# Attention on one NeuronCore: the value product of a group in one TensorE run instead of two

## The chip, the cores and the metric

The kernel runs on one core of a Trainium2 chip. The metric is device time in microseconds (us) from launch to end. The kernel before took 1688.72 us, the median of three runs (1685.79 to 1690.38). One further execution was taken with the hardware profiler; all durations below come from it.

The engines are TensorE (PE, matmuls; its weight loads are shown as PEld), VectorE (DVE), ScalarE (ACT), GpSimd (POOL) and SyncE (SP, which here only issues transfers). TensorE writes to PSUM, eight banks of 512 float32 columns on 128 partitions. DVE and ACT read it there.

## The reference

One layer in float32: cross attention, a sparsified gated feed-forward part, and a low-rank mixture of experts, each with a layer norm before it and a residual. The change is in the cross attention:

```python
xq = q.reshape(b, s, N_KV_HEADS, N_REP, HEAD_DIM)        # 16 x 64 tokens, 8 x 4 heads of 32
scores = jnp.einsum('bsgrd,btgd->bgrst', xq, xk) / math.sqrt(HEAD_DIM)   # t = 1601
probs = jax.nn.softmax((scores + mask).astype(jnp.float32), axis=-1)
out = jnp.einsum('bgrst,btgd->bsgrd', probs, xv)
x = x + out
```

Here q is the layer norm of x, and keys and values are both the context. The feed-forward part has a width of 2752 and keeps the larger half of the gate's magnitudes; eight experts of rank 16 follow, two per token.

## The kernel before

**Groups.** Attention is cut into 64 groups: batch element b (16), half h of the eight key heads (2), half rh of the four query heads that share a key head (2). A group has four key heads g, each of 32 dimensions. For each the 128 partitions of a score tile are 2 query heads x 64 tokens, and the columns are the 1601 context rows. Eight groups (two batch elements) use one tile of 128 tokens; the index of a group inside its tile is m.

**Steps of a group** (class `Group`). `scores(d)` computes half d of the columns (0 to 801, 801 to 1601) for the four heads as eight matmuls: a part of 512 columns for each head, then a part of 289 or 288. The four heads lie on different 32-row strips of the array and stream side by side. Seven results go to banks of the pool `ps_t`, which has seven and hands them out in rotation; the last goes to the bank `shared`. `masked(d)` is eight DVE operations that add the mask and write to SBUF, with a running maximum; each is followed by a short read of the accumulator. After d=1 a reduction makes the negative maximum `nm`. `softmax(g)` is one ACT exponent over 1601 columns with its sum. `turn(heads)` transposes the probabilities of two heads on TensorE, 26 blocks in seven banks of `ps_t`, and returns the seven copies from PSUM to SBUF (`pT`) for the caller to place on ACT or DVE. `values(d)` multiplies transposed probabilities with values: 13 blocks of context rows times four heads on 32-column strips. In the trace each float32 matmul shows as two weight loads and two matmul records, so 104 records for a group. The result `po` is the last 128 columns of the bank `shared`. `keep(d)` copies `po` into `oT` on DVE (d=0) or adds it there (d=1). `inverse` takes the reciprocals of the sums.

**Order.** `InOrder` (line 88) keeps each engine's operations in the order in which the program calls them, so the loop over groups sets every queue by hand. Its helper is line 96, which is why almost all rows of the profile carry L96. In iteration n, for d = 0 and 1, the calls are: scores(d) of group n+1, values(d) of group n-1, masked(d) of n+1, turn of two heads of group n with copies 0, 1, 2, 3 and 5 on ACT and 4 and 6 on DVE, keep(d) of n-1, and two exponents (heads 2 and 3 of n in d=0, heads 0 and 1 of n+1 in d=1). TensorE thus repeats: scores, values, transposes, scores, values, transposes. `values(0)` takes six blocks, `values(1)` seven.

**Beside it.** On SP stand the loads of keys and values (`load_kv`, at the first score run of every fourth group), of the next tile of x (m=2) and its queries (m=3), and the store of a finished tile (m=4). `Norm` computes a token tile's statistics on DVE, half of it at each d of m=4; `row_tile` sends them through DRAM and `scale_queries` (POOL, m=5) makes the queries. `finish_tile` transposes `oT` back and adds it to x. POOL also forms sums of weight blocks, one of 48 units per group. The feed-forward part behind is ordered by a planner (`Plan`) with its own costs. It calls the last group's values, keep and inverse first.

Of the kernel before, what the change touches and what calls it, by code (L numbers as in the profile page):

```python
# [9 lines left out]
F32 = mybir.dt.float32  # L10
# [6 lines left out]
ALU = mybir.AluOpType  # L17
# [3 lines left out]
P = 128  # L21
B, S, D = 16, 64, 1024
T, C = 1601, 256
HD = 32
# [3 lines left out]

HALVES = [(0, 801), (801, T)]
BANK = 512  # L30
LOADS = [(0, 512), (512, 801), (801, T)]
NCH = 4
I = 2752
IC = 344
# [22 lines left out]
def tile_perceiver_layer(  # L57
# [120 lines left out]
    def sums_out(u):  # L178
        (_, t), _ = sum_columns(u)
        pool.dma_start(t, sums[u])  # L180

    def load_x(i, parts=1):
        x[i] = xp.tile([P, D], F32, tag="x", name=f"x{i}")
        for j in range(parts):
            cols = slice(j * D // parts, (j + 1) * D // parts)
            sp_queue.dma_start(x[i][:, cols], x_in[i * P : (i + 1) * P, cols])
# [76 lines left out]
    class Group:  # L263
# [7 lines left out]
        def scores(self, d):  # L271


            b, h, rh = self.b, self.h, self.rh
            if d == 0:
                self.sc = [
                    scp.tile([P, T], F32, tag=f"sc{g}", name=f"sc{g}_{self.name}")
                    for g in range(4)
                ]
                self.mx = small.tile([P, 4, NCH], F32, tag="mx", name=f"mx_{self.name}")  # L280
                self.sums = small.tile([P, 4], F32, tag="sums", name=f"sums_{self.name}")
                if (h, rh) == (0, 1) and b + 1 < B:
                    load_kv(b + 1)
            t0, t1 = HALVES[d]
            mid = t0 + BANK
            self.parts = []
            for j in range(8):
                g, (c0, c1) = j % 4, ((t0, mid), (mid, t1))[j // 4]
                bank = shared
                if j < 7:  # L290
                    bank = ps_t.tile([P, BANK], F32, tag="pt", name=f"ps{j}_{self.name}_{d}")
                ps = bank[:, : c1 - c0]
                rows = slice(g * HD, (g + 1) * HD)
                q = qT[b // 2][rows, h, b % 2, 2 * rh : 2 * rh + 2, :]
                pe.matmul(
                    ps,
                    q.rearrange("p r s -> p (r s)"),
                    kv[b][0][h][rows, c0:c1],
                    start=True,
                    stop=True,  # L300
                )
                self.parts.append((g, c0, c1, ps, 2 * d + j // 4))

        def masked(self, d):

# [40 lines left out]
            copies.append((pT[:TL, :, last, :], pt[:TL]))  # L346
            return copies

        def values(self, d):


            c0, c1 = ((0, NTC // 2), (NTC // 2, NTC), (0, NTC))[d]
            v = kv[self.b][1][self.h]
            for c in range(c0, c1):
                w = min(P, T - c * P)
                for g in range(4):
                    pe.matmul(
                        po[g * HD : (g + 1) * HD, :],
                        v[:w, c, g * HD : (g + 1) * HD],
                        self.pT[g][:w, c, :],  # L360
                        start=(c == c0),
                        stop=(c == c1 - 1),
                    )

        def keep(self, d):

            i, bb = self.b // 2, self.b % 2
            if bb == 0 and self.h == 0 and self.rh == 0 and d != 1:
                oT[i] = otp.tile([P, 2, 4, 2, S], F32, tag="oT", name=f"oT{i}")
                rs_tok[i] = small.tile([P, 2, 4, 4], F32, tag="rs", name=f"rs{i}")  # L370
            rows = oT[i][:, self.h, 2 * self.rh : 2 * self.rh + 2, bb, :]
            new = po.rearrange("p (r s) -> p r s", r=2)
            if d == 1:
                dve.tensor_tensor(rows, new, rows, ALU.add)
            else:
                dve.tensor_copy(rows, new)

        def inverse(self):

# [9 lines left out]
    def finish_tile(i, h, home=ps_t, tag="pt"):  # L389


        if h == 0:
            att[i] = xnp.tile([P, 2, 4, 4, HD], F32, tag="xn", name=f"att{i}")
        rows = att[i][:, h]
        pt = home.tile([P, 4, P], F32, tag=tag, name=f"pto{i}_{h}")
        for r in range(4):
            pe.transpose(
                pt[:, r, :], oT[i][:, h, r].rearrange("p b s -> p (b s)"), ident
            )

        def add():
            pool.tensor_tensor(
                rows, rows, rs_tok[i][:, h].unsqueeze(3).to_broadcast([P, 4, 4, HD]),
                ALU.mult,
            )
            xv = x[i].rearrange("p (h g r d) -> p h r g d", h=2, g=4, r=4)
            pool.tensor_tensor(xv[:, h], xv[:, h], rows, ALU.add)

        return (rows, pt.rearrange("p r (g d) -> p r g d", g=4)), add
# [24 lines left out]
    for d in range(2):  # L434
# [1 line left out]
        for _ in range(4):  # L436
            pe.transpose(po, ident, ident)
        groups[0].masked(d)
    for g in range(2):
        groups[0].softmax(g)  # L440


    first, first_xn = (xnp, otp), {}
    for n in range(ng):
        i, m = n // 8 + 1, n % 8
        group = groups[n]
        last = n == ng - 1
        if m == 2 and i < NT:
            load_x(i)
        if m == 3 and i < NT:  # L450
            raw = load_queries(i)
        if m == 4 and n > 8:
            sp_queue.dma_start(xs[i - 2], x[i - 2])
        if n == ng - 3:
            for j in range(2):
                x[j] = xp.tile([P, D], F32, tag="x", name=f"x{j}_f")
                sp_queue.dma_start(x[j], xs[j])
        for d in range(2):
            add = None
            following = groups[n + 1] if not last else None  # L460
            if following:
                following.scores(d)
            if n > 0:
                groups[n - 1].values(d)
            if following:
                following.masked(d)
            on_act = [0, 1, 2] if last else [0, 1, 2, 3, 5]
            if n > 8 and 3 <= 2 * m + d <= 4:
                copy, add = finish_tile(i - 2, 1 - d)
                act.copy(*copy)  # L470
            if last:
                groups[n - 1].keep(d)
            copies = group.turn((2 * d, 2 * d + 1))
            for j, copy in enumerate(copies):
                if j in on_act:
                    act.copy(*copy)
                else:
                    dve.tensor_copy(*copy)
            if n > 0:
                if not last:  # L480
                    groups[n - 1].keep(d)
                if d == 1:
                    groups[n - 1].inverse()
            for g in range(2):
                if d == 0:
                    group.softmax(2 + g)
                elif following:
                    following.softmax(g)
            if add:
                add()  # L490
            if i < NT:
                if (m, d) == (4, 0):
                    norm = Norm(x[i], f"q{i}", float(HD))
                if m == 4:
                    norm.half(d)
                if (m, d) == (4, 1):
                    norm.end()
                    row = row_tile(i)
                if (m, d) == (5, 1):
                    scale_queries(i, raw, row)  # L500
            if d == 1 and 0 <= n - 3 < 3 * NU:
                sums_made(n - 3)
                sums_out(n - 3)
            if d == 1 and 0 <= n - 2 < 3 * NU:
                sums_in(n - 2)
            if last:
                xn = first[d].tile([P, D], F32, tag=("xn", "oT")[d], name=f"xn_f{d}")
                norm = Norm(x[d], f"f{d}")
                norm.half(0)
                norm.half(1)  # L510
                norm.end()
                dve.tensor_scalar(xn, x[d], norm.mean, norm.rstd, ALU.subtract, ALU.mult)
                first_xn[d] = xn

# [748 lines left out]
    rank = {name: 10 + 10 * j for j, name in enumerate(order)}  # L1265
    gated = [gate(pairs[0], 0, rank["g0"], lambda i: [])]

    t = add("PE", 2.9, lambda: groups[-1].values(2), [], rank["g0"] - 5)
    t = add("DVE", 0.3, lambda: groups[-1].keep(2), [t], 0)
    t = add("DVE", 0.4, lambda: groups[-1].inverse(), [t], 0)  # L1270

    def end():
# [44 lines left out]
class Plan:  # L1317
# [20 lines left out]
    def add(self, engine, cost, emit, deps, rank, takes=None, frees=None, margin=0.0):  # L1338
        holds, frees = (
            [hold for hold in (h if isinstance(h, tuple) else (h,)) if hold]  # L1340
            for h in (takes, frees)
        )
        task = self.Task(engine, cost, emit, deps, rank, holds, margin)
        for hold in frees:
            hold.freed_by = task
        self.tasks.append(task)
        return task
# [102 lines left out]
```

## Time and profile before

| | |
|---|---|
| median of three runs | 1688.72 us |
| the profiled execution's own time | 1688.13 us |
| its span, first to last instruction | 1686.2 us |
| attention, up to the first gate matmul | 814.65 us |
| one group in the steady state | 12.21 us |
| PE, DVE, ACT, POOL busy in 300 to 400 us | 99.95, 90.97, 96.00, 52.71 us |
| granted TensorE clock in that stretch | 1.00 |

A row of the timeline gives the start, the duration, the engine, the line, the operation, output <- input, the shape, and the number of instructions merged into it; in brackets stands the idle time before it and what ended it. PE rows are named by what they write: `ps<-kT,qt` and `shared<-kT,qt` are scores, `shared<-pT,v` values, `pt<-ident,sc` transposes, `pto` the transposes of `finish_tile`. Matmuls are pipelined and their ends modelled, so the distance from one run's start to the next tells more than a duration. ACT's `sc<-sc,nm` is an exponent, `pT<-pt` a copy of transposed probabilities, DVE's `sc<-ps,mask` a masking, `oT<-shared` the work of `keep`.

### The profile page before, as it was taken

What the parts mean: (1) busy time and instruction counts of PE and PEld (TensorE: products, weight loads), DVE (VectorE), ACT (ScalarE), POOL (GpSimd) and SP (SyncE); (2) the same over time, 40 slices, a digit from 0 to 9 for tenths busy, and PEclk for the clock granted to TensorE, in tenths of its full rate; (3) what the DMA queues carried; (4) which work ended last, traced back from release to release, by engine and by line L of the source; (5) the groups of instructions that cost most, each with busy time, mean ns of one, the idle gap of its engine ahead of it and who ended that gap; (6) DMA issues with size and microseconds to landing.
All of it is one profiled execution on the core that took longest, in us unless ns stands there. A gap on an engine that the chain in (4) does not pass through costs nothing. (4 is left out here: it accounts for less than half of the span.)

```text
span 1686.2 us, 38279 instructions
## 1 busy us (share of the span) xinstructions
PE 1662.9 (99%) x15042; PEld 1184.2 (70%) x15042; DVE 1437.8 (85%) x3654; ACT 1257.1 (75%) x1702; POOL 573.9 (34%) x613
## 2 busy tenths in 40 slices
PE   8999999999999999999999999999989999999998
PEld 7888888888888888888666666645645656645644
DVE  7998989999898999988439999999999989999603
ACT  6999999999999999999256675778477772877010
POOL 1055555455554554110221212221480013420631
PEclk9999999999999999999999999999999999999999
DMA  7356657565664766131799999888959979898983
GB/s 220 105 160 202 216 159 228 190 229 169 217 209 155 229 209 201 46 98 49 309 303 327 300 300 305 283 289 266 347 185 302 310 233 328 268 298 270 315 267 133
DMA packets 133586, 389.11 MB, mean 231 GB/s; under 512 B 9888, under 2 KB 61376, under 8 KB 133408
## 3 DMA queue, kind: packets, MB, share of 16 engines
q1 hardware_dynamic: 113840, 315.98, 57.4%
q0 software_dynamic: 19136, 69.61, 12.5%
q8 instruction: 119, 1.95, 0.5%
q10 hardware_dynamic: 432, 1.09, 0.2%
q14 instruction: 59, 0.48, 0.1%
HBM read 344.17 MB, written 42.47 MB: 229 GB/s over the span
## 5 line engine op out<-in xcount | busy, mean ns | idle before, releaser
L96 DVE CUSTOM_DVE_ANT_0 sc<-ps,mask 128x512 f32<-128x512 f32 (+2 forms) x896 | 468.4, 588 | 31.2 <-PE ps L96 30.0
L96 ACT ACTIVATE sign<-a,cand 128x2752 int8<-128x2752 f32 x136 | 351.8, 2587 | 111.5 <-DVE cand L96 111.4
L96 ACT ACTIVATE sc<-sc,nm 128x1601 f32<-128x1601 f32 x256 | 415.7, 1629 | 8.8 <-DVE nm L96 8.8
L96 PE MATMUL pt<-ident,sc 128*128 128x128 f32 (+1 forms) x3328 | 395.1, 275 | 2.1 <-ACT sc L96 1.7
L96 DVE TENSOR_SCALAR_CACHE_REDUCE junk<-a,cand 128x2752 uint8<-128x2752 f32 x124 | 381.7, 3078 | 4.0
L96 PEld LDWEIGHTS pt<-ident,sc 128*128 128x128 f32 (+1 forms) x3328 | 362.7, 141 | 28.4 <-issue 23.8
L96 ACT COPY pT<-pt 128x512 f32<-128x512 f32 x636 | 336.4, 598 | 29.4 <-PE pt L96 17.8
L96 PE MATMUL pg_u<-w_u,hS 128*128 128x344 f32 x896 | 263.4, 452 | 0.0
L96 PE MATMUL pg_g<-w_g,hS 128*128 128x344 f32 x896 | 261.0, 452 | 0.8 <-DVE hS L96 0.8
L96 POOL TENSOR_TENSOR tw<-tw 128x344 f32<-128x344 f32 (+1 forms) x192 | 176.0, 927 | 223.2 <-DMA tw<-in_wg_dram 74.5
L96 PE MATMUL pd<-w_d,s 128*128 128x512 f32 x528 | 234.6, 598 | 0.0
L96 PEld LDWEIGHTS pg_g<-w_g,hS 128*128 128x128 f32 x896 | 169.6, 190 | 88.9 <-DVE hS L96 1.0
L96 PEld LDWEIGHTS pg_u<-w_u,hS 128*128 128x128 f32 x896 | 168.8, 190 | 87.3 <-issue 3.1
L96 PE MATMUL ps<-kT,qt 32*128 32x512 f32 (+2 forms) x1792 | 209.8, 538 | 1.0 <-DVE mx L96 0.9
L96 PE MATMUL shared<-pT,v 128*32 128x128 f32 x6656 | 208.5, 274 | 0.9 <-DVE oT L96 0.7
L96 PEld LDWEIGHTS shared<-pT,v 128*32 128x32 f32 x6656 | 174.2, 110 | 49.6 <-issue 48.0
L96 PEld LDWEIGHTS pd<-w_d,s 128*128 128x128 f32 x528 | 99.6, 193 | 115.7 <-issue 114.8
L96 DVE COPY pT<-pt 128x512 f32<-128x512 f32 (+1 forms) x260 | 139.5, 558 | 38.9 <-PE pt L96 38.9
L96 PEld LDWEIGHTS ps<-kT,qt 32*128 32x128 f32 x1792 | 97.6, 183 | 53.3 <-DVE pT L96 27.8
L96 ACT ACTIVATE s<-s 128x344 f32<-128x344 f32 (+1 forms) x70 | 36.6, 536 | 74.9 <-DVE s L96 74.7
L96 POOL TENSOR_TENSOR s<-s,rank 128x688 f32<-128x688 f32 x32 | 62.4, 1964 | 77.5 <-DVE rank L96 76.9
L96 DVE DVE_READ_ACCUMULATOR2_ANT mx<- 128x1 f32 x1024 | 84.8, 83 | 0.0
(331 smaller groups left out, 1403.2 us busy)
## 6 DMA issues: line engine op xcount, KB each, us to landing
w_g<-ts SPq DMA_DIRECT2D x64, 688.0 KB
w_u<-ts SPq DMA_DIRECT2D x64, 688.0 KB
w_d<-ts SPq DMA_DIRECT2D x48, 768.0 KB
w_g<-in_wg_dram SPq DMA_DIRECT2D x48, 688.0 KB
w_u<-in_wu_dram SPq DMA_DIRECT2D x48, 688.0 KB
w_d<-in_wd_dram SPq DMA_DIRECT2D x36, 768.0 KB
kT<-in_ctx_t_dram SPq DMA_DIRECT2D x31, 800.5 KB
v<-in_ctx_v_dram SPq DMA_DIRECT2D x32, 768.0 KB
```

The lines of the kernel that those rows point to most:

```text
L96: return tc.keep_in_program_order(getattr(self.engine, op)(*args, **kwargs))
```

## The change

- `values` covers all 13 blocks in one call and accumulates them in PSUM; `keep` is one copy, without the addition.
- Order in iteration n: scores(1) and masked(1) of group n+1; turn of heads 2 and 3 of group n; values, keep and inverse of group n; exponents 0, 1 and 2 of n+1; then `next_group(n + 1)`: scores(0) and masked(0) of n+2, turn of heads 0 and 1 of n+1, exponent 3 of n+1. TensorE repeats scores, transposes, values, scores, transposes.
- Copies: of heads 0 and 1, the first six on ACT and the seventh on DVE; of heads 2 and 3, the first four on ACT and three on DVE. In the last group every other one is on ACT.
- In `scores` the parts of 289 or 288 columns come first. The fourth of these goes to `shared`; it is masked last.
- `Norm` of the next tile runs in one piece at m=3, the queries are scaled at m=4; x is loaded at m=1; queries are loaded, and the finished tile is stored, at m=2; `finish_tile` runs at m=0 and 1. The statistics of the first two feed-forward tiles run in the last group but one. The first transfers load columns 512 to 801 ahead of 0 to 512.

```diff
-LOADS = [(0, 512), (512, 801), (801, T)]
+LOADS = [(512, 801), (0, 512), (801, T)]
...
-                g, (c0, c1) = j % 4, ((t0, mid), (mid, t1))[j // 4]
+                g, k, (c0, c1) = j % 4, j // 4, ((mid, t1), (t0, mid))[j // 4]
                 bank = shared
-                if j < 7:
+                if j != 3:
                     bank = ps_t.tile([P, BANK], F32, tag="pt", name=f"ps{j}_{self.name}_{d}")
...
+            self.parts.append(self.parts.pop(3))
...
-            c0, c1 = ((0, NTC // 2), (NTC // 2, NTC), (0, NTC))[d]
             v = kv[self.b][1][self.h]
-            for c in range(c0, c1):
+            for c in range(NTC):
...
-            if d == 1:
-                dve.tensor_tensor(rows, new, rows, ALU.add)
-            else:
-                dve.tensor_copy(rows, new)
+            dve.tensor_copy(
+                oT[i][:, self.h, 2 * self.rh : 2 * self.rh + 2, bb, :],
+                po.rearrange("p (r s) -> p r s", r=2),
+            )
...
+    def next_group(n):
+        if n + 1 < ng:
+            groups[n + 1].scores(0)
+            groups[n + 1].masked(0)
+        turn_and_copy(groups[n], (0, 1), (0, 1, 2, 3, 4, 5))
+        groups[n].softmax(3)
...
+        if following:
+            following.scores(1)
+            following.masked(1)
+        if n >= 8 and m < 2:
+            copy, add = finish_tile(i - 2, m)
+            act.copy(*copy)
+        turn_and_copy(group, (2, 3), (0, 1, 2, 3) if following else (0, 2, 4, 6))
+        if following:
+            group.values()
+            group.keep()
+            group.inverse()
+            for g in range(3):
+                following.softmax(g)
+            next_group(n + 1)
+        if add:
+            add()
+        if i < NT and m == 3:
+            norm = Norm(x[i], f"q{i}", float(HD))
+            for j in range(2):
+                norm.half(j)
+            norm.end()
+            row = row_tile(i)
+        if i < NT and m == 4:
+            scale_queries(i, raw, row)
```

More of the change, by code (lines that the diff above doesn't have):

```diff
@@ L301, in scores @@
                 )
-                self.parts.append((g, c0, c1, ps, 2 * d + j // 4))
+                self.parts.append((g, c0, c1, ps, 2 * d + k))
+            self.parts.append(self.parts.pop(3))
         def masked(self, d):
@@ L347, in turn, with values @@
             return copies
-        def values(self, d):
-            c0, c1 = ((0, NTC // 2), (NTC // 2, NTC), (0, NTC))[d]
+        def values(self):
             v = kv[self.b][1][self.h]
-            for c in range(c0, c1):
+            for c in range(NTC):
                 w = min(P, T - c * P)
@@ L360, in values, with keep @@
                         self.pT[g][:w, c, :],
-                        start=(c == c0),
-                        stop=(c == c1 - 1),
+                        start=(c == 0),
+                        stop=(c == NTC - 1),
                     )
-        def keep(self, d):
+        def keep(self):
             i, bb = self.b // 2, self.b % 2
-            if bb == 0 and self.h == 0 and self.rh == 0 and d != 1:
+            if bb == 0 and self.h == 0 and self.rh == 0:
                 oT[i] = otp.tile([P, 2, 4, 2, S], F32, tag="oT", name=f"oT{i}")
                 rs_tok[i] = small.tile([P, 2, 4, 4], F32, tag="rs", name=f"rs{i}")
-            rows = oT[i][:, self.h, 2 * self.rh : 2 * self.rh + 2, bb, :]
-            new = po.rearrange("p (r s) -> p r s", r=2)
-            if d == 1:
-                dve.tensor_tensor(rows, new, rows, ALU.add)
-            else:
-                dve.tensor_copy(rows, new)
+            dve.tensor_copy(
+                oT[i][:, self.h, 2 * self.rh : 2 * self.rh + 2, bb, :],
+                po.rearrange("p (r s) -> p r s", r=2),
+            )
         def inverse(self):
@@ L438, in tile_perceiver_layer, with turn_and_copy @@
         groups[0].masked(d)
-    for g in range(2):
+    for g in range(3):
         groups[0].softmax(g)
+    def turn_and_copy(group, heads, on_act):
+        for j, copy in enumerate(group.turn(heads)):
+            if j in on_act:
+                act.copy(*copy)
+            else:
+                dve.tensor_copy(*copy)
+    def next_group(n):
[4 more added lines that the diff above has]
+        groups[n].softmax(3)
+    next_group(0)
     first, first_xn = (xnp, otp), {}
@@ L445, in tile_perceiver_layer @@
         i, m = n // 8 + 1, n % 8
-        group = groups[n]
-        last = n == ng - 1
+        group, add = groups[n], None
+        following = groups[n + 1] if n + 1 < ng else None
+        if m == 1 and i < NT:
+            load_x(i)
+        if m == 2 and n > 8:
+            sp_queue.dma_start(xs[i - 2], x[i - 2])
         if m == 2 and i < NT:
-            load_x(i)
-        if m == 3 and i < NT:
             raw = load_queries(i)
-        if m == 4 and n > 8:
-            sp_queue.dma_start(xs[i - 2], x[i - 2])
         if n == ng - 3:
@@ L457, in tile_perceiver_layer @@
                 sp_queue.dma_start(x[j], xs[j])
[L458 to L508, printed above, removed]
@@ new lines, in tile_perceiver_layer @@
+        if following:
[3 more added lines that the diff above has]
+            copy, add = finish_tile(i - 2, m)
+            act.copy(*copy)
+        turn_and_copy(group, (2, 3), (0, 1, 2, 3) if following else (0, 2, 4, 6))
[3 more added lines that the diff above has]
+            group.inverse()
+            for g in range(3):
+                following.softmax(g)
+            next_group(n + 1)
+        if add:
+            add()
@@ new lines, in tile_perceiver_layer @@
+        if i < NT and m == 3:
[6 more added lines that the diff above has]
+            scale_queries(i, raw, row)
+        if 0 <= n - 3 < 3 * NU:
+            sums_made(n - 3)
+            sums_out(n - 3)
+        if 0 <= n - 2 < 3 * NU:
+            sums_in(n - 2)
+        if n == ng - 2:
+            for j in range(2):
+                xn = first[j].tile([P, D], F32, tag=("xn", "oT")[j], name=f"xn_f{j}")
+                norm = Norm(x[j], f"f{j}")
@@ L511, in tile_perceiver_layer @@
                 norm.end()
-                dve.tensor_scalar(xn, x[d], norm.mean, norm.rstd, ALU.subtract, ALU.mult)
-                first_xn[d] = xn
+                dve.tensor_scalar(xn, x[j], norm.mean, norm.rstd, ALU.subtract, ALU.mult)
+                first_xn[j] = xn
     early.close()
@@ L1266, in tile_perceiver_layer @@
     gated = [gate(pairs[0], 0, rank["g0"], lambda i: [])]
-    t = add("PE", 2.9, lambda: groups[-1].values(2), [], rank["g0"] - 5)
-    t = add("DVE", 0.3, lambda: groups[-1].keep(2), [t], 0)
+    t = add("PE", 2.9, lambda: groups[-1].values(), [], rank["g0"] - 5)
+    t = add("DVE", 0.3, lambda: groups[-1].keep(), [t], 0)
     t = add("DVE", 0.4, lambda: groups[-1].inverse(), [t], 0)
```

## The prediction

> **What bounds the kernel now.** I read the page's busy shares first, then busy time by stage, then the timeline of one group, and last the waits. The change lies in attention, which ends with the first gate matmul at 814.65 us; the feed-forward part behind it keeps its code. Busy time in a stretch of 100 us inside attention (columns: PE, weight loads, DVE, ACT, POOL, granted clock, DMA share, GB/s):
>
> ```profile
> PE 1662.9 (99%) x15042; PEld 1184.2 (70%) x15042; DVE 1437.8 (85%) x3654; ACT 1257.1 (75%) x1702; POOL 573.9 (34%) x613
> ...
> 300.00:400.00 100.00, 99.95 (x1524) 83.52 (x1522) 90.97 (x336) 96.00 (x150) 52.71 (x60) 1.00 0.61 200
> ```
>
> TensorE has no idle time, ACT and DVE have little, DMA has plenty. Busy PE alone proves nothing, so here is one group's timeline (start, duration, engine, operation):
>
> ```profile
> 301.16 1.38 PE L96 MATMUL ps<-kT,qt 32*128 32x512 f32 x11
> ...
> 301.61 0.28 DVE L96 TENSOR_TENSOR oT<-shared,oT 128x128 f32<-128x128 f32 x1
> ...
> 301.94 0.18 PEld L96 LDWEIGHTS shared<-kT,qt 32*128 32x128 f32 x1
> ...
> 302.15 0.40 PE L96 MATMUL shared<-kT,qt 32*128 32x289 f32 x1
> ...
> 302.39 0.40 PE L96 MATMUL shared<-kT,qt 32*128 32x289 f32 x1
> 302.72 1.25 PEld L96 LDWEIGHTS shared<-pT,v 128*32 128x32 f32 x48 [0.39 <-issue]
> 302.72 1.52 PE L96 MATMUL shared<-pT,v 128*32 128x128 f32 x48
> ...
> 304.17 3.06 PE L96 MATMUL pt<-ident,sc 128*128 128x128 f32 x26
> ...
> 307.16 1.38 PE L96 MATMUL ps<-kT,qt 32*128 32x512 f32 x11
> ...
> 308.72 1.74 PE L96 MATMUL shared<-pT,v 128*32 128x128 f32 x56
> ...
> 310.38 3.06 PE L96 MATMUL pt<-ident,sc 128*128 128x128 f32 x26
> ...
> 311.13 2.71 ACT L96 COPY pT<-pt 128x512 f32<-128x512 f32 x5 [0.27 <-PE pt L96]
> ...
> 313.37 1.38 PE L96 MATMUL ps<-kT,qt 32*128 32x512 f32 x11
> ```
>
> Start to start: scores 1.56 us, values 1.45 (48 records) or 1.66 to 1.67 (56), transposes 2.99; a group is 12.21 us (301.16 to 313.37), in six runs. The same run lengths return group after group, so no run waits for data: TensorE's own stream is the bound. The copy of the value result (oT<-shared) runs during the next score run, and the score matmul that needs its bank comes last there: it loads weights at 301.94 and streams at 302.15, on time. This copy is hidden now.
>
> Three rows from elsewhere give the prices. The first two are the end of attention, where nothing stood between a value run and its copy; the third is a row of five ACT copies without a wait:
>
> ```profile
> 796.21 1.52 PE L96 MATMUL shared<-pT,v 128*32 128x128 f32 x48 [0.71 <-DVE oT L96]
> ...
> 797.79 0.29 DVE L96 COPY oT<-shared 128x128 f32<-128x128 f32 x1 [1.25 <-PE shared L96]
> ```
>
> ```profile
> 27.60 2.51 ACT L96 COPY pT<-pt 128x512 f32<-128x512 f32 x5
> ```
>
> **The change, part by part.** Per group TensorE's order becomes: scores d=1 of the next group, transposes of heads 2 and 3, all values, scores d=0 of the group after, transposes of heads 0 and 1.
>
> *One value run instead of two.* 56 records against 48 cost 1.67 - 1.45 = 0.22 us, 0.0275 a record, so 48 cost 1.32 and a run has 0.13 us of its own. One run less: -0.13. Bounds: 0, and -0.19 (from the rounding of the starts). The saved add into oT (0.28 us of DVE) is worth nothing while DVE idles 9 us in 100.
>
> *Values right before scores d=0.* The score part in `shared` is now in the first four, not the last, and `shared` holds the value result that `keep` must copy out. In the row above the run after the values started at 797.66 and the copy at 797.79, 0.13 later, for 0.29; the weight load came 0.05 after such a copy (301.61+0.28 to 301.94). So head 3's weights come 0.47 after the run's start, against 0.02 for a fourth head: +0.45. Its row group then streams short and long part one after the other, so nothing catches up, and the next transposes, which use the whole array, wait for it. Queued behind it: the transposes, then all else on PE. Bounds: 0, if the copy were still covered; 0.47+0.24=0.71, if the second four also waited for its first pass (0.24, 302.15 to 302.39). I take 0.45: in the prologue a score matmul of another row group started at 12.28 while a late one's second pass began only at 12.44, so row groups stream independently.
>
> *Six ACT copies behind transposes 0/1, before scores d=1.* The first ACT copy starts 0.75 after the transposes (310.38 to 311.13), five take 2.51 with a mean of 0.60, so one follows another after (2.51-0.60)/4=0.48. The sixth ends 0.75+5x0.48+0.60=3.75 after the transposes start, and releases 0.05 later the bank of the seventh score matmul: 0.81 into a run that starts at 2.99. That matmul should stream at 0.59 (0.11 entry, two short passes of 0.24); with weights loaded for 0.10 after 0.81 it does at 0.91: +0.32. The entry is the excess of a run's first long pass over its second, 0.53 against 0.43 in the single records (301.16, 301.70, 302.13); a late weight load costs the same. Bounds: 0 (a DVE copy would have kept pace; before, copies 4 and 6 are DVE's) and 0.80 (ACT 0.48 late throughout). I take 0.33, the row's own figure with rounding.
>
> *ACT and DVE as bounds.* ACT: four exponents at 1.63, ten copies at 0.48, two restarts of 0.24 after an exponent: 11.8 of the new period. DVE falls. Neither binds at 12.86. The third exponent ahead of the copies and the fourth behind them have cover: values and scores d=0 (about 5 us) run between.
>
> Net per group: -0.13+0.45+0.33 = **+0.65 us**, period 12.86. Over the 62 groups that have the full pattern: +40.3.
>
> *Statistics of the next token tile, in one piece.* Seven times per kernel two bn_stats (0.69 each), an aggregate (0.21) and a scalar (0.15), less overlap 1.65 us, now stand before the masks of scores d=1 in DVE's queue. DVE is free 0.45 into the score run, so masks begin at 2.1 instead of about 0.8. Transposes wait for the first mask to free their bank: 2.1+0.45+0.05=2.6 against 1.89, +0.7. Their last bank waits for the last long mask: 2.1+3x0.38+4x0.61+0.15=5.8 against 2.6+2.7=5.3, +0.5 to 0.6. Together 1.3; before, the two halves lay apart and cost one 3.43 instead of 3.06 transposes run, 0.37. 7 x 0.93 = +6.5. Bounds: 0 and 7x1.65=11.6.
>
> *Fill and end.* Values of group 0 move one group earlier: +3.0 (2.86+0.13) in the first groups. At the end a value run leaves, but TensorE waits there for the last group's exponents anyway, so nothing returns. Bounds: 0 and 5.
>
> *Moved transfers.* The x load, the query load and the store of x each stand one or two groups earlier or the same on SP's queue, behind the same key and value loads. DMA is 61% busy here, and the query scaling on POOL (four at 1.3 us) has two groups of cover; without it a tile would wait some 5 us. The first loads swap order, with the same bytes; the first scores wait for the queries (8.16 us). I take 0. The feed-forward part: 0; its first weight load is issued at 794.44, 20 us ahead of its first matmul, and the same steps follow it.
>
> Sum: 40.3+6.5+3.0 = +49.8 on the profiled execution's 1688.13 us (span 1686.2; 0.6 below the median of the three runs): **1738 us**.
>
> *A rule against the saved run.* The row: 99.95 of 100 us of PE busy, and score, value and transpose runs that never vary in length. The Trainium skill ("Trainium Kernel Development and Optimization", Performance Expectations) says matmul busy time misleads and weight-load busy tells the distance to the limit. By that, 83.5 of 100 leaves TensorE room, a saved run is worth 0, and the sum would be 62x0.78+9.5, 1746 us. I keep the row's figure, because the fixed 0.13 us is itself time in which neither streams.
>
> **Rivals.**
>
> *Faster.* One mechanism: the banks come back in time, so the saved run is all that is left. For it: TensorE's stream is the bound today, and DVE and ACT have 9 and 4 us in 100 free. Then 62x(-0.13) = -8, +3 fill: 1683. It decides if both stalls together stay under 0.1 us a group. Against: nothing stands between values and `shared`, so 0.45 is a sum of three observed latencies. 5%.
>
> *Only the shared bank stalls*, ACT keeping pace with its six copies: 62x0.32+9.5 = +29, 1717. For: ACT's copies run at 0.48 against 0.44 for four transposes, a narrow miss. 15%.
>
> *Only the copies stall*, `keep` hidden: 62x0.20+9.5=+22, 1710. 7%.
>
> *ACT becomes the bound.* Late copies delay the fourth exponent, and with it the transposes of head 3; 11.8 us of ACT work plus 1.5 of new waits is 13.3: 62x1.1+9.5=+78, 1766. For: its 96% today. Against: a period of 12.86 gives it a full microsecond. 8%.
>
> **How the numbers follow.** The forecast holds 65%: 1738, with its own range 1728 to 1748. The range, 1715 to 1753, takes in the shared-bank case and part of the ACT one and leaves out the faster case, the copies-alone case and the far ACT one. About 0.3% is what a measurement can tell from no change. Faster has its 0.05; 0.02 of the copies-alone case, where that stall shrinks too, lies within it; the rest, 0.93, is slower.
>
> **What would show it.** In the profile after: value runs of 104 records and 2.98 us, five runs a group, a period of 12.8 to 12.9; score runs of 1.9 to 2.0 us instead of 1.56, the weight load of `shared` waiting for DVE's oT after each value run, and the seventh score load waiting for ACT's pT. A transposes run near 3.6 and a score run near 2.7 once per tile. Wrong would be the whole if score runs kept 1.56, or if the period were over 13.2 with ACT idle nowhere.

## The result and the profile after

The changed kernel takes 1741.88 us, the median of six runs (1738.25 to 1745.75), against 1689.12 for the kernel before beside it: ratio 1.0317, 95% interval 1.0298 to 1.0336. It is slower by 53 us. The profiled execution took 1745.52 us, with a span of 1743.7; the one of before took 1688.13, so the two traces differ by 57.4.

The busy times of the page, and of the stretch from 300 to 400 us (columns as in the table of before):

```profile
PE 1713.1 (98%) x15042; PEld 1196.9 (69%) x15042; DVE 1417.4 (81%) x3587; ACT 1252.2 (72%) x1706; POOL 575.9 (33%) x613
```

```profile
300.00:400.00 100.00, 99.39 (x1393) 80.15 (x1392) 84.19 (x312) 89.56 (x142) 52.97 (x59) 1.00 0.58 190
```

TensorE is still shown as busy for 99.39 of 100 us, but with 1393 matmul records instead of 1524: each group takes longer. How many records a stretch holds depends on which runs it cuts; the mean of the five stretches from 100 to 600 us is 1444 against 1530. No other engine is near its limit; ACT, at 96.00 before, now idles 10 us in 100. Where the time goes is in the timeline of one group of the changed kernel:

```profile
310.81 0.76 PE L96 MATMUL ps<-kT,qt 32*128 32x289 f32 x6
310.94 0.29 DVE L96 COPY oT<-shared 128x128 f32<-128x128 f32 x1 [1.45 <-PE shared L96]
311.29 0.18 PEld L96 LDWEIGHTS shared<-kT,qt 32*128 32x128 f32 x1 [0.18 <-DVE oT L96]
...
311.64 0.40 PE L96 MATMUL shared<-kT,qt 32*128 32x289 f32 x1
...
312.83 3.06 PE L96 MATMUL pt<-ident,sc 128*128 128x128 f32 x26
313.58 3.03 ACT L96 COPY pT<-pt 128x512 f32<-128x512 f32 x6 [0.56 <-PE pt L96]
...
315.82 0.52 PE L96 MATMUL ps<-kT,qt 32*128 32x288 f32 x3
...
317.72 3.06 PE L96 MATMUL pt<-ident,sc 128*128 128x128 f32 x26
...
320.71 3.05 PE L96 MATMUL shared<-pT,v 128*32 128x128 f32 x104
...
323.69 0.52 PE L96 MATMUL ps<-kT,qt 32*128 32x289 f32 x3
```

Start to start: scores d=0 2.02 us, transposes 2.99, scores d=1 1.90, transposes 2.99, values 2.98; a group is 12.88 us (310.81 to 323.69). Before it was 12.21. Both score runs are longer than 1.56, and each for a reason that the rows show.

In the first, the copy of the value result starts 0.13 us into the score run and takes 0.29; the weight load of `shared` follows at 311.29, 0.48 into the run. In the second, the sixth of ACT's copies ends at 313.58 + 3.03 = 316.61. A finer look at the weight loads of the same run shows the pair for heads 2 and 3 of the long parts right behind it, 0.84 into a run that started at 315.82:

```profile
316.66 0.19 PEld L96 LDWEIGHTS ps<-kT,qt 32*128 32x128 f32 x2
```

The waits of the changed kernel from 200 to 600 us (us in total, times, longest) have the first of these about once for each of the 31 groups; the kernel before has no row of `oT` there.

```profile
DVE oT L96 <- PE shared L96: 48.5, 31, 1.9
PEld shared L96 <- DVE oT L96: 5.5, 31, 0.2
```

The group with the statistics of the next tile is the longest, 14.15 us, because the masks stand behind them in DVE's queue and the transposes wait for the masks:

```profile
78.88 1.27 DVE L96 BATCH_NORM_STATS2 st_q<-x 128x6 f32<-128x512 f32 x2
...
80.50 0.45 DVE L96 CUSTOM_DVE_ANT_0 sc<-ps,mask 128x288 f32<-128x288 f32 x1
...
81.01 3.63 PE L96 MATMUL pt<-ident,sc 128*128 128x128 f32 x26 [0.61 <-DVE mx L96]
```

The first gate matmul starts at 872.22 us instead of 814.65. What lies behind it takes 871.5 us in both. All of the loss is in attention.

### The profile page after: what moved, and what is told of

Same layout as the page of the kernel before. It is cut to its first block, busy times and chain, and to the rows that moved or that the text cites. A ratio compares the mean times of both kernels' runs of the same rounds, so it can differ in the third digit from the quotient of the medians.

```text
span 1743.7 us, 38195 instructions
## 1 busy us (share of the span) xinstructions
PE 1713.1 (98%) x15042; PEld 1196.9 (69%) x15042; DVE 1417.4 (81%) x3587; ACT 1252.2 (72%) x1706; POOL 575.9 (33%) x613
## 4 chain that ended last, share of the span: by engine, by line
PE 81%; DVE 11%; issue 3%; POOL 2%; ACT 2%; DMA 1%; SPq 0%; DVEq 0%; ACTq 0%; POOLq 0%
PE pt L96 22%; PE ps L96 12%; PE shared L96 12%; PE pg_g L96 12%; PE pg_u L96 11%; PE pd L96 9%; DVE junk L96 6%; POOL s L96 2%; ACT sign L96 1%; DVE rank L96 1%; PE py L96 1%; DVE s L96 1%; DVE sc L96 1%; PE pl L96 1%; DVE st_q L96 0%
## 5 line engine op out<-in xcount | busy, mean ns | idle before, releaser
L96 ACT COPY pT<-pt 128x512 f32<-128x512 f32 x640 | 325.9, 607 | 61.3 <-PE pt L96 61.1
L96 PE MATMUL ps<-kT,qt 32*128 32x512 f32 (+2 forms) x1792 | 264.3, 543 | 2.1 <-DVE mx L96 1.0
L96 PE MATMUL shared<-pT,v 128*32 128x128 f32 x6656 | 197.6, 275 | 1.7 <-DVE pT L96 1.7
L96 PEld LDWEIGHTS shared<-pT,v 128*32 128x32 f32 x6656 | 179.7, 111 | 13.7 <-DVE mx L96 8.5
L96 PEld LDWEIGHTS ps<-kT,qt 32*128 32x128 f32 x1792 | 125.8, 184 | 44.2 <-issue 12.7
L96 DVE COPY pT<-pt 128x512 f32<-128x512 f32 (+1 forms) x256 | 129.9, 549 | 24.0 <-PE pt L96 23.8
L96 DVE COPY oT<-shared 128x128 f32<-128x128 f32 x64 | 18.7, 292 | 101.9 <-PE shared L96 101.9
L96 PE MATMUL shared<-kT,qt 32*128 32x289 f32 (+1 forms) x256 | 96.5, 456 | 1.5 <-DVE mx L96 1.5
```

The costliest lines, as they stand in the source:

```text
L96: return tc.keep_in_program_order(getattr(self.engine, op)(*args, **kwargs))
```

## The experiments

Two theories were held against each other. **A** is the prediction's way of adding up: each late bank has a price of its own, and taking it away gives the price back. **B** says that the second value run was more than work: it was the time in which DVE and ACT emptied the banks and finished exponents, and without it a wait that is removed at one place comes back at the next.

### Undo one thing: `shared` last again

```diff
-                if j != 3:
+                if j < 7:
...
-            self.parts.append(self.parts.pop(3))
```

> The changed kernel with one thing undone: the score part in the bank shared is again the last of the eight (head 3's long part), so the copy of the value result has until the second four to finish. Theory A (the prediction's sum, each stall with its own price): score runs d=0 go from 2.02 back to 1.56 us, all other runs stay, the period goes from 12.88 to 12.42, and 61 groups x -0.46 give about 1714 us. Theory B (the banks are drained too slowly in the stretch of scores, transposes, scores, transposes that lies between two value runs, so a wait that goes in one run comes back in a later one): DVE can begin its masks only after that copy (0.13 + 0.29 into the score run) and two reciprocals (0.36), at about 0.85; the seventh of the masks in program order (four short at 0.38, three long at 0.61) frees its bank at about 4.3, while the transposes now want it at 1.56 + 2.64 = 4.2; transposes of both kinds become 3.05 to 3.1, score runs d=1 stay above 1.8, the period is 12.5 to 12.6 and the time 1718 to 1725 us.

Measured: 1722.17 us, ratio to before 1.0197 (1.018 to 1.0214). The price of the copy in the score run is real: 20 us of the 53 go with it. But the period of the plain groups is 12.51 to 12.57, not 12.42. Runs, start to start: scores d=0 1.56, transposes 3.09, scores d=1 1.82, transposes 3.07, values 2.98. The timeline of this kernel:

```profile
301.73 1.19 PE L96 MATMUL ps<-kT,qt 32*128 32x289 f32 x11
301.87 0.29 DVE L96 COPY oT<-shared 128x128 f32<-128x128 f32 x1 [1.44 <-PE shared L96]
302.22 0.18 PEld L96 LDWEIGHTS shared<-kT,qt 32*128 32x128 f32 x1
...
302.58 0.46 DVE L96 CUSTOM_DVE_ANT_0 sc<-ps,mask 128x289 f32<-128x289 f32 x1
...
306.08 0.19 PEld L96 LDWEIGHTS pt<-ident,sc 128*65 128x65 f32 x2 [0.18 <-DVE mx L96]
```

The copy is hidden, but the masks begin 0.85 us into the score run as before, and the last two transposes wait for one of them (306.08). B, with the size that it gave: of the 0.46 taken away, the period shows some 0.35.

### Deal the copies as before

```diff
-        turn_and_copy(groups[n], (0, 1), (0, 1, 2, 3, 4, 5))
+        turn_and_copy(groups[n], (0, 1), (0, 1, 2, 3, 5))
```

> The changed kernel with the copies of transposes 0/1 dealt as in the kernel before: five on ACT, the fifth and the seventh on DVE. Theory A (the prediction: six copies on ACT in a row are what makes the seventh score matmul late, a DVE copy would have kept pace): score runs d=1 go from 1.90 to 1.56 us, the period to 12.54, the time to about 1721 us. Theory B (draining of banks): DVE's masks of scores d=0 begin about 0.83 into that run and take 4 x 0.38 + 4 x 0.61 = 3.96, so they end 2.8 us into the transposes; DVE's two copies end at about 3.4 and 3.9, no sooner than ACT's sixth at 3.75: score runs d=1 keep 1.9 us, the period 12.9, the time 1740 to 1746 us.

Measured: 1743.09 us, 1.0322 (1.0306 to 1.0337), no different from the changed kernel. Scores d=1 take 1.86 to 1.93 us in the plain groups, the period is 12.87 to 12.91. DVE reaches its two copies only after its masks. The timeline of this kernel, from the start of the transposes at 300.00:

```profile
302.41 0.46 DVE L96 CUSTOM_DVE_ANT_0 sc<-shared,mask 128x289 f32<-128x289 f32 x1
302.79 1.01 DVE L96 COPY pT<-pt 128x512 f32<-128x512 f32 x2
```

Its second copy ends at 302.79 + 1.01 = 303.80, and the weight load of the last score part in the run that started at 302.98 comes 0.05 behind it:

```profile
303.85 0.18 PEld L96 LDWEIGHTS ps<-kT,qt 32*128 32x128 f32 x1
```

So the sixth copy on ACT was what held the bank in the changed kernel, and still it was not a mistake of the deal: the other engine has no time there. B.

### One part alone: the kernel before with a joined value run

```diff
-            if n > 0:
-                groups[n - 1].values(d)
+            if n > 0 and (last or d == 0):
+                groups[n - 1].values(d if last else 2)
...
-                if not last:
-                    groups[n - 1].keep(d)
+                if not last and d == 0:
+                    groups[n - 1].keep(2)
```

> The kernel before with one part of the change alone: the values of a group in one run (13 blocks, after scores d=0 of the next group), one keep, everything else as before. Theory A (the prediction's first term: a run less is worth 0.13, and the copy of the value result stays hidden, because shared is the last score part here): period 12.21 - 0.13 = 12.08, 62 x -0.13 = -8, about 1681 us. By the rule of the Trainium skill that was weighed in the prediction, 0. Theory B (the value run is also the pause in which DVE and ACT empty the score banks before the transposes of heads 2 and 3 want them; joined, one of the two pauses is gone): transposes of heads 2 and 3 go from 2.99 to 3.3 us or more, score runs from 1.56 to 1.9 or more, the period is over 12.8 us and the time over 1725 us.

Measured: 1747.10 us, 1.0348 (1.0332 to 1.0363). The value run takes 2.98 us, 0.14 less than the two did, as A and the prediction have it. Everything else gives back eight times as much: score runs 1.74 and 2.15, transposes of heads 2 and 3 3.34, period 13.20. B has the size, but its words named the score banks, and the weight loads of these transposes wait for something else:

```profile
280.40 1.41 PEld L96 LDWEIGHTS pt<-ident,sc 128*128 128x128 f32 x12 [0.97 <-ACT sc L96]
282.06 1.51 PEld L96 LDWEIGHTS pt<-ident,sc 128*128 128x128 f32 x14 [0.26 <-ACT sc L96]
```

ACT does the exponents of heads 2 and 3 behind its copies of transposes 0/1. The value run that stood between was their cover.

### The joined run with the exponents ahead

```diff
-            for g in range(2):
-                if d == 0:
-                    group.softmax(2 + g)
-                elif following:
-                    following.softmax(g)
+            if d == 0:
+                group.softmax(3)
+            elif following:
+                for g in range(3):
+                    following.softmax(g)
```

> The kernel before with the joined value run of e3_join, and the exponents dealt as in the changed kernel: three right after scores d=1 (while TensorE runs scores d=0 and the values), the fourth behind the copies of transposes 0/1. In e3_join (1747 us, period 13.20) the transposes of heads 2 and 3 waited for ACT's exponents of these heads, because the value run that had stood ahead of them was gone. Theory A (that wait is the whole loss): these transposes return to 2.99 us, score runs to 1.56 to 1.9, the period to 12.1 to 12.5 and the time to 1681 to 1706 us. Theory B (with the exponent in time the next thing is late, the masks of scores d=1: DVE is busy with two copies and keep until 1.1 us into that score run, then each long mask takes 0.61, while the transposes want a bank every 0.44 from 1.6 us on): the transposes take 3.4 to 3.6 us, the score runs 1.7 to 2.0, the period is 12.9 to 13.2 and the time 1730 to 1750 us.

Measured: 1737.72 us, 1.0294 (1.0278 to 1.031), period 13.04, these transposes 3.57 us, score runs 1.58 and 1.91. The exponents are no longer waited for. The waits of this kernel from 200 to 600 us now have the masks at the head of TensorE's weight loads:

```profile
PEld pt L96 <- DVE mx L96: 31.7, 90, 0.8
```

B, here with its mechanism too: behind the exponents stood the masks. (The score runs of 1.58 lie below B's range; the transposes and the period are in it.) Joining the value run alone is a loss of 1 us a group, and dealing the exponents anew returns 0.16 of it.

### Short parts first, alone

```diff
-                g, (c0, c1) = j % 4, ((t0, mid), (mid, t1))[j // 4]
+                g, (c0, c1) = j % 4, ((mid, t1), (t0, mid))[j // 4]
```

> The kernel before with one part of the change alone: the score parts of 289 columns are issued ahead of those of 512; shared stays the last of the eight. Theory A (only where a bank is late does the order matter, and before no run waits): the score runs keep 1.56 us, the time stays at 1688 us within 0.3%. Theory B (short parts first means that the fifth to seventh bank are asked for about 0.5 into the run instead of 0.9, while the copies that free them come at the same pace): score runs lengthen to 1.8 to 1.9 us, twice a group, the period becomes about 12.8 us and the time 1720 to 1728 us. In the changed kernel the same order would then have a share in the 0.34 us that scores d=1 lost.

In this kernel head 3's long part fills the bank `shared`, and the value run overwrites its last 128 columns before they are masked; it has the same instructions. Measured: 1720.41 us, 1.0183 (1.0168 to 1.0198); score runs 1.83, period 12.76. The size is B's, the mechanism is not. These are DVE's and then TensorE's rows in one score run of this kernel, which starts at 202.39:

```profile
201.84 1.08 DVE L96 COPY pT<-pt 128x512 f32<-128x512 f32 x2 [0.52 <-PE pt L96]
202.84 0.28 DVE L96 COPY oT<-shared 128x128 f32<-128x128 f32 x1
```

```profile
202.39 0.88 PEld L96 LDWEIGHTS ps<-kT,qt 32*128 32x128 f32 x14 [0.17 <-ACT pT L96]
203.17 0.29 PEld L96 LDWEIGHTS shared<-kT,qt 32*128 32x128 f32 x2
```

The weights of `shared` come at 0.78, 0.05 behind `keep` (202.84 + 0.28 = 203.12). A second part streams at 0.59 if its weights are there 0.1 earlier, so this one is 0.29 late. The sixth and seventh part of `ps` load at 0.53 and 0.58, behind DVE's copies, and are late by less than 0.1. One more kernel tells the two apart:

```diff
-                g, (c0, c1) = j % 4, ((t0, mid), (mid, t1))[j // 4]
+                g, k = j % 4, (j // 4 + (j % 4 == 3)) % 2
+                c0, c1 = ((mid, t1), (t0, mid))[k]
```

> The kernel before, short score parts first for heads 0 to 2 and long first for head 3, so that the bank shared gets head 3's short part, last of the eight. In e4_short (1720 us) shared had a long part, wanted about 0.5 us into the score run, and its weights were loaded at 0.78, right after keep. Theory A (that wait alone made the score runs of e4_short 1.83 us): here the part in shared is wanted at about 0.96 as in the kernel before, the score runs are 1.56 to 1.65 us, the time 1687 to 1702 us. Theory B (the fifth to seventh bank, wanted at 0.5, are late as well): score runs 1.8 us or more, 1718 us or more.

Measured: 1697.48 us, 1.0046 (1.0028 to 1.0064); score runs 1.63, period 12.36. Theory A of this run: three quarters of the loss of short parts first was the wait for `shared`. In this kernel its weights come 0.78 into the run as well, but now nothing needs them sooner:

```profile
203.87 0.88 PEld L96 LDWEIGHTS ps<-kT,qt 32*128 32x128 f32 x14 [0.17 <-issue]
204.65 0.39 PEld L96 LDWEIGHTS shared<-kT,qt 32*128 32x128 f32 x2
```

The 0.07 per run that stay fit the small delay of the sixth and seventh part; that was not tried alone.

### Long parts first in the new order

```diff
-                g, k, (c0, c1) = j % 4, j // 4, ((mid, t1), (t0, mid))[j // 4]
+                g, k, (c0, c1) = j % 4, j // 4, ((t0, mid), (mid, t1))[j // 4]
...
-                if j != 3:
+                if j < 7:
...
-            self.parts.append(self.parts.pop(3))
```

> The changed kernel with long score parts first, as in the kernel before; shared is then the last part again (head 3's short one). To be read against e1_last (1722 us, period 12.5), which differs in the order of the parts alone. Theory A (short parts first cost 0.27 us in each score run, as in e4_short): score runs 1.56 us, period about 12.1 to 12.2, about 1700 us. Theory B (in the new order transposes follow a score run at once, with no value run between; their first bank is free when the first mask is through, and four long masks of 0.61 come first instead of four short ones of 0.38): transposes of both kinds go from about 3.05 to 3.4 to 3.6 us and the rest is handed on to the score runs; the period is over 13.3 us and the time over 1770 us.

Measured: 1802.80 us, 1.068 (1.0663 to 1.0698), the slowest of all; period 13.95, transposes 3.48 and 3.57, score runs 1.91 and 2.00. Against the first experiment, whose parts are short first, that is 81 us. B. The weight loads of one transposes run show the pace of the long masks, one every 0.61 us (297.22, 297.83, 298.44):

```profile
297.22 0.42 PEld L96 LDWEIGHTS pt<-ident,sc 128*128 128x128 f32 x4 [0.74 <-DVE mx L96]
...
297.83 0.42 PEld L96 LDWEIGHTS pt<-ident,sc 128*128 128x128 f32 x4 [0.19 <-DVE mx L96]
...
298.44 0.42 PEld L96 LDWEIGHTS pt<-ident,sc 128*128 128x128 f32 x4 [0.19 <-DVE mx L96]
```

So the order of the parts has no fixed price. With a value run behind each score run, short parts first cost time, three quarters of it because `shared` becomes urgent; with transposes behind, they are what lets the transposes start.

### The statistics in another gap

```diff
+        if i < NT and m == 2:
+            norm = Norm(x[i], f"q{i}", float(HD))
+            norm.half(0)
+        if i < NT and m == 3:
+            norm.half(1)
+            norm.end()
+            row = row_tile(i)
         if following:
             group.values()
...
-        if i < NT and m == 3:
-            norm = Norm(x[i], f"q{i}", float(HD))
-            for j in range(2):
-                norm.half(j)
-            norm.end()
-            row = row_tile(i)
```

> The changed kernel with the statistics of the next token tile moved alone: one half at m=2, the other half and the end at m=3, each issued ahead of keep, where DVE idles 1.45 us per group waiting for the value run, instead of all of it ahead of the masks of scores d=1. Theory A (the term of the prediction): the seven groups of 14.15 us become 12.88 like the others, 7 x -1.27 = -9, about 1733 us. Theory B (DVE's copies of transposes 2/3, the statistics and keep stand in one queue, and keep is late by them): score runs d=0 at m=2 and 3 become longer than 2.02 by 0.3 or more, the gain is under 4 us, 1738 us or more.

Measured: 1733.57 us, 1.027 (1.0246 to 1.0294): 8.3 less than the changed kernel. The groups at m=2 and 3 take 12.88 like the others; score runs d=0 there keep 2.02. A. The same move on top of the first experiment:

> e1_last (shared last again) and e7_norm together: the best version of the new order that these experiments give. If the two are independent: 1722 - 9 = 1713 us, still 24 us over the kernel before; if DVE is so late in e1_last that the statistics have no idle time there: 1718 us or more.

Measured: 1712.36 us, 1.0143 (1.0122 to 1.0163). The two add up. It is the best of the versions with the new order and still some 25 us above the kernel before.

### The instruction stream shifted

The last experiment is about something else. In the profiled execution five groups between 600 and 790 us took 0.3 to 0.9 us more than their like. One of them, in the changed kernel:

```profile
613.47 0.31 PEld L96 LDWEIGHTS ps<-kT,qt 32*128 32x128 f32 x6 [0.20 <-issue]
...
615.29 0.31 PEld L96 LDWEIGHTS ps<-kT,qt 32*128 32x128 f32 x8 [1.05 <-PE shared L96]
```

Nothing that the row could wait for was late: these banks come free during the value run. A 16 KB transfer of instructions had started at 612.62.

```diff
-    for _ in range(24):
+    for _ in range(72):
         pe.transpose(warm[:, 0, :], ident, ident)
```

> The changed kernel with 72 instead of 24 of the transposes that precede the first queries: 48 more, 96 records of TensorE ahead of everything, some 5 us more in the opening. Nothing else differs. In the profile of the changed kernel score runs d=0 at 613.5, 640.1, 667.3 and 694.3 us (groups 46 to 52) pause for 0.3 to 1.0 us, each right after a 16 KB transfer of instructions that began 390 records or more behind the one before. Theory A (an instruction block arrives late where its boundary falls at the end of a value run): with the boundaries moved by 96 records, the pauses stand in other groups or are gone. Theory B (something of the data in these groups): the same groups pause.

Measured: 1745.79 us in one run. None of the groups pauses, there or elsewhere: from the third group on all take 12.88, 13.32 (with `finish_tile`) or 14.15. The third group's scores start 4.0 us later than in the changed kernel, and the pauses, 3.3 us, are gone, as theory A has it. But each kernel was profiled in one execution, and the pauses are not fixed: the kernels with the copies dealt as before and with the statistics moved, whose TensorE program is that of the changed kernel, pause for 1.8 and 0.8 us in theirs, each in two of the same five groups. So A is supported and not shown.

## Why the prediction was right

Forecast were 1738 us and slower, with 0.93; measured were 1741.88 and slower. By its terms, in the two profiled executions:

| term | forecast, us | measured, us |
|---|---|---|
| value run, per group | -0.13 | -0.14 |
| scores d=0, per group | +0.45 | +0.46 |
| scores d=1, per group | +0.33 | +0.34 |
| groups: 62 x 0.65 forecast, 61 x (12.88 - 12.21) measured | +40.3 | +40.9 |
| statistics, 7 x | +6.5 | +6.1 |
| opening, up to the third group's scores | +3.0 | +5.3 |
| pauses in the five groups | 0 | +3.3 |
| end, last scores d=0 to the first gate matmul | 0 | +2.0 |
| feed-forward part | 0 | 0.0 |
| sum | +49.8 | +57.6 |

**The saved run.** 2.98 against 1.45 + 1.67: the row's figure, -0.14, and not the 0 of the rule on weight-load time that was weighed against it. A page that was not drawn on then fits: the Trainium skill ("TensorEngine Tiling (Array Packing)", Key Properties) says that a change of tiling mode drains TensorE, and a run less is a change less. That the 0.14 us were the price of this drain, no run here shows.

**The two late banks.** Both sit where they were forecast, and both are shown: the weight load of `shared` 0.06 behind the end of DVE's copy, the load of the seventh score part 0.05 behind the end of ACT's sixth copy, and experiments that move either. The wait for `shared` does not come from shared columns: the short part takes 289 of the bank and the value result the last 128. The Trainium skill ("PSUM — Partial Sum Buffer", PSUM bank collisions raise a hardware error) asks for a guard by bank and quadrant, not by address. No run here tried it without.

**Statistics.** The score run of these groups takes 2.58 (forecast 2.6) and the transposes 3.58, in all 1.27 over the others (forecast 1.3); moved away, they cost nothing.

**What failed.** The prediction said of the sixth copy "Bounds: 0 (a DVE copy would have kept pace)". It would not: dealt so, the time is the same. It also treated the two late banks as prices that can be taken off one by one, as in its rivals "only the shared bank stalls" and "only the copies stall". They don't add up that way: 0.46 taken away returned 0.35. This did no harm, because both were there. For the end of attention it said that "nothing returns"; in the profiled execution 2.0 us were lost there.

**The rivals.** Faster: the banks did not come back in time. ACT as the bound: it idles 10 us in 100. Single stalls: both were there.

**The deeper reason** was not in the prediction. It took the value run for work that lies in the stream, and asked what its removal saves. The joined run in the otherwise old kernel costs 58 us, since a value run needs no bank of `ps_t`: while it ran, ACT finished exponents and DVE emptied score banks. The rest of the change (three exponents ahead, short parts first, copies dealt anew) lowers that loss but did not make up for the second pause in any version here.

The median differs from the forecast by 4 us, the profiled execution by 7.5. In that execution the opening, the pauses and the end came to 10.6 us where 3.0 were forecast. These three terms vary: the kernel with the statistics moved has the same TensorE program and, in the opening and in the end, the same instructions on every engine; in its profiled execution the three came to 2.7, 0.8 and 0.2 us. So the +3.0 for the opening and the 0 for the end were not wrong in kind; what the prediction left out is that such stretches can be several us longer in one execution than in another.

## What to carry to other kernels

A run on the bounding engine that takes nothing from a shared buffer pool is also the time in which the other engines catch up; before joining two such runs, list what each engine finishes under each of them and what would ask for it next. A late buffer has a price only together with the next one in line, so after taking a wait away, look for the row that comes up late in its place. Work that must go somewhere on a queue belongs where its engine waits for the bounding engine anyway: the statistics cost 6 us more than before ahead of the masks, and nothing ahead of `keep`.

## What was not expected of the hardware

**Pauses beside instruction transfers.** TensorE's instructions arrive in blocks of 16 KB, 119 in the changed kernel. Six of them between 600 and 790 us started 388 to 450 records of TensorE after the one before, where the mean is 257 (30619 records, those of semaphores included, in 119 blocks); in five of the six cases the group was longer, by up to 0.9 us. The Trainium skill ("Runtime: NRT & Kernel Launch", Instruction fetch mechanics) calls the crossing of a block boundary mostly hidden. Here TensorE paused beside it a few times in an execution, and in the one profiled execution with the stream shifted by 96 records it did not. That the late blocks are the cause is argued from this alone. A late block is not enough: in the shifted kernel one came 415 records after the last, at 144.5 us, and in the kernel with the statistics moved one 457 records after the last, at 760.1 us, both without a pause. What else it takes stays open. In the profile of the first experiment's kernel one group took 16.54 us instead of 12.86, and the granted clock was half for 3.4 us of it; which of the two came of the other is not shown.

**The clock fell back in the opening.** The granted clock in the stretches 13 to 20 and 20 to 27 us (the third figure from the right, ahead of DMA share and GB/s) was half in the changed kernel, and 0.98 and 0.77 in the kernel before; first the changed kernel, then the one before:

```profile
13.00:20.00 7.00, 6.31 (x29) 2.92 (x24) 5.34 (x23) 1.60 (x2) 0.00 (x0) 0.52 1.13 317
20.00:27.00 7.00, 7.00 (x35) 5.49 (x30) 2.91 (x10) 6.35 (x12) 0.00 (x0) 0.51 0.48 155
```

```profile
13.00:20.00 7.00, 5.79 (x33) 3.72 (x30) 6.97 (x28) 2.44 (x3) 3.27 (x4) 0.98 1.17 321
20.00:27.00 7.00, 6.48 (x47) 5.42 (x45) 4.41 (x17) 6.14 (x10) 1.89 (x3) 0.77 0.99 325
```

The transposes there took 5.74 us instead of 4.65. The kernel with the statistics moved runs the same instructions in its opening as the changed kernel, and in its profile the clock was half for 3.4 us instead of 13.7:

```profile
13.00:20.00 7.00, 5.40 (x35) 2.99 (x36) 6.88 (x28) 2.74 (x3) 0.00 (x0) 0.94 1.14 324
20.00:27.00 7.00, 7.00 (x46) 5.50 (x45) 4.13 (x18) 6.82 (x13) 0.00 (x0) 0.82 0.44 146
```

Its third group's scores start at 32.18 us, those of the changed kernel at 34.78. So the 2.3 us by which the opening was forecast too low go with the longer slow stretch of that execution. The end has another such stretch, 860 to 867 us at 0.53, in which 98 of the 104 records of a value run take 4.89 us. What decides the length of these stretches stays open; no experiment was made on it.
